# Turning the attention's normalized rows of blocks 2 to 15 on VectorE in squares of 32, from permuted row tiles, with a gather inside SBUF

## The chip, the cores and the metric

The kernel runs on one core of one Trainium2 chip, in float32. The metric is the device time of one execution in microseconds; the time of a kernel is the median of several executions. All five engines of the core are in use: TensorE (PE, with its weight loads PEld), VectorE (DVE), ScalarE (ACT), GpSimd (POOL), and SyncE (SP), which issues nearly all DMAs.

## What is computed

One transformer block with adaptive layer norm, on x of 8 × 1024 × 512 (16 heads of 32) with a condition of 8 × 512. Cut to what matters:

```python
mod = jax.nn.silu(condition) @ Wada + bada
sh_a, sc_a, gt_a, sh_m, sc_m, gt_m = jnp.split(mod, 6, axis=1)
xn = _layernorm(x, g1, be1)
xm = xn * (1.0 + sc_a[:, None, :]) + sh_a[:, None, :]
x = x + gt_a[:, None, :] * _attention(xm, Wqkv, Wproj, bproj)
xn = _layernorm(x, g2, be2)
xm = xn * (1.0 + sc_m[:, None, :]) + sh_m[:, None, :]
h = jax.nn.gelu(xm @ W1 + b1, approximate=False)
x = x + gt_m[:, None, :] * (h @ W2 + b2)
```

The attention is causal. What the change touches is the path from x to the first `xm`: x arrives as rows of tokens, the layer norm's statistics need a token's 512 values in one partition, and the products q, k and v need the 512 values along the partitions. So the normalized rows have to be transposed.

## The kernel before

**Tiling.** The 8192 tokens are 16 blocks of 512, half a sequence each. A block's rows are four row tiles (`hat`, 128 tokens × 512 values), which become four column chunks (`xm[:, c, :]`, 128 values × 512 tokens). The large products (qkv, up, down, proj) use seven products of halves in place of eight; their combinations are named as in the code. Of the attention's input they are B11, B21 and B22 (quarters of `xm`), T1 (written over the fourth quarter) and T2, T3, T4 (three parts of a second tile, `t`). Of a weight they are A11, S1 and so on, 256 KB each. Each of the seven products of a block is 16 matmuls in L205, written as 32 or 64 records in the trace.

**Order.** The kernel writes its own instruction order. A planner runs along while the program is built: it keeps a clock for every engine (`now`), the time at which each piece of data will be there (`written`) and each buffer will be free (`left`). A `note(engine, ns, reads, writes)` advances a clock. `plan` lists the steps of each of the stages; the linear products form the main stream, the attention runs beside it, and side threads opened with `start(...)` are taken up when what they `yield` on is due by the planner's clocks. `either` and `sooner` choose an engine in the same way. On the chip each engine then runs its instructions strictly in that order, each waiting for the semaphores of what it needs. `costs` gives the share of PE's time that a step is expected to take, by which the attention's work is paced.

**Weights.** SP fetches them in a fixed order into a ring of nine tiles `w` (`fetch`, `release`): a fetch goes out when a product releases the tile that it overwrites. In the profile these are L342 (a quarter of a raw weight) and L344 (a sum kept in DRAM). The same queue carries the loads of x (L384 for `hat`, L1230 for the residual) and the stores of the result (L1070).

**The part that is changed.** Step `load_xa` loads four row tiles of a block with four DMAs, `norm_a` takes the statistics (L568 on DVE) and normalizes in place (L594 on ACT; L589 on DVE for two tiles of block 0). Step `at` opens the side thread `modulated`: for each chunk, PE transposes four 128 × 128 squares into a PSUM bank (L656), and DVE (L660) or ACT (L666) applies gain and shift on the way from the bank to `xm`. Then come T1 (L673), T2 (L675) and, through `either` (L162 on DVE, L165 on POOL), T3 and T4. `mt` does the same for the second layer norm, from tiles `xh`, and is not changed. For blocks 2 to 15 `at` stands in the plan behind a part of an up or down product of an earlier block: the attention's input is made ready ahead of its use.

**Around it.** In blocks 4 to 15 the thread runs while the down product of another block ends. Its last combinations on DVE are u2 (then `u2 += b2_rows`), u3 and y21, each the evacuation of one product from its bank (L197). After it come the seven products of v (`project_v`), the first of which, p1, is copied out of its bank by ACT (L192). u3 lives in a buffer of tag "p1", which v's p1 uses next; u3 is read by y21:

```python
u3 = stage("u3", "p1")
combine_out(u3, bank, ps, u2, [key("u2")], [key("u3")])
...
y = stage("y21", "y", 2)
combine_out(y, bank, ps, u3, [key("u3")], [key("y21")])
```

The linear products share three PSUM banks (`lin_bank`); a product needs a bank whose last content was copied out.

Of the kernel before, what the change touches and what calls it, by code (L numbers as in the profile page):

```python
# [9 lines left out]
F32 = mybir.dt.float32  # L10
BF16 = mybir.dt.bfloat16
AF = mybir.ActivationFunctionType
# [10 lines left out]
def kernel(  # L23
# [33 lines left out]
    nc = tc.nc  # L57
    B, T, D = x.shape
    HD = W1.shape[1]
    P = 128  # L60
    hd = D // H
    scale = float(hd) ** -0.5
    TB = 512
    NTT = TB // P
    NHALF = T // TB
    NC = D // P
# [28 lines left out]
    written, left = {}, {}  # L95
# [16 lines left out]
    def note(engine, ns, reads=(), writes=(), port=False):  # L112
        start = max(now[engine], due(reads, writes))
        if port:
            start = max([start] + [b for a, b in pool_spans if a <= start < b])
        end = start + ns
        now[engine] = end
        if engine == "POOL":
            pool_spans.append((start, end))
            del pool_spans[:-16]  # L120
        for k in reads:
            left[k] = max(left.get(k, 0.0), end + SYNC)
        for k in writes:
            written[k] = end + SYNC
        return end

    def note_pe(ns, form, reads=(), writes=()):
        now["PE"] = max(now["PE"], due(reads, writes))
        if shape[0] != form:
            shape[0] = form  # L130
            now["PE"] += SWITCH
        note("PE", ns, reads)
        spent[0] += ns
        for k in writes:
            written[k] = now["PE"] + PIPE

    def note_act(ns, func, reads=(), writes=()):
        if func is not None and table[0] != func:
            table[0] = func
            ns += TABLE  # L140
        note("ACT", ns, reads, writes)
# [5 lines left out]
    def sooner(reads, writes, dve, act):  # L147

        t = due(reads, writes)
        return "DVE" if max(now["DVE"], t) + dve <= max(now["ACT"], t) + act else "ACT"  # L150
# [26 lines left out]
    def lin_bank():  # L177
        i = min(
            (i for i in range(3) if not live[i]),
            key=lambda i: left.get(("l", i), 0.0),  # L180
        )
        live[i] = True
        return i
# [30 lines left out]
    TR = 108  # L214
# [106 lines left out]

    order = [at for w in range(-1, NB + 1) for step in plan[w] for at in pieces_of(step)]
    costs = {"at": 16 * TR, "mt": 16 * TR, "gates": 4 * MM, "mod": 32 * TR}
    costs.update({kind: 14 * MM for kind in ("k", "q", "v", "u", "proj")})

    def planned_time(w):
# [22 lines left out]
    def take(count):  # L349
        i = taken[0]  # L350
        taken[0] += count
        return list(range(i, taken[0]))
# [10 lines left out]
    def halves(i):  # L363
        return piece(i).rearrange("p (k n) -> p k n", n=HB)
# [11 lines left out]
        r0 += n  # L376
    O_G1, O_BE1, O_G2, O_BE2, O_BPROJ, O_B1, O_BADA = at

    def load_x(n, pool, tag):
        b, h = blocks[n]  # L380
        tiles = []
        for t in range(NTT):
            xt = pool.tile([P, D], F32, tag=tag, name=f"{tag}_{n}_{t}", bufs=NTT)
            nc.sync.dma_start(xt, x[b, h * TB + t * P : h * TB + (t + 1) * P, :])  # L384
            tiles.append(xt)
        return tiles

    x_pre = {0: load_x(0, tmp, "hat")}
# [7 lines left out]
        make_causal_mask(nc, mask[:, ts(i, P)], MASKED)  # L396
    eps = const.tile([P, 1], F32, tag="eps", name="eps")
    nc.gpsimd.memset(eps, EPS)
    ones = const.tile([P, P], F32, tag="ones", name="ones")
    nc.gpsimd.memset(ones, 1.0)  # L400
    minus_ones = const.tile([P, P], BF16, tag="minus_ones", name="minus_ones")
    nc.gpsimd.memset(minus_ones, -1.0)
# [66 lines left out]
    def gates(kind):  # L469

        i, bias = GATES[kind]
        at = take(4)
        part = {kf: halves(j) for kf, j in zip(RAW, at)}
        b_gate = tmp.tile([P, D], F32, tag="y", name=f"b_gate_{kind}")[:B, :]
        nc.sync.dma_start(b_gate, bada[i * D : (i + 1) * D].unsqueeze(0).to_broadcast([B, D]))
        if bias is not None:
            b_out = tmp.tile([P, D], F32, tag="y", name=f"b_out_{kind}")[:B, :]
            nc.sync.dma_start(b_out, bias.unsqueeze(0).to_broadcast([B, D]))
        yield [], [BANK]
        bank = lin_bank()  # L480
        ps = banks[bank][:B, :]
        for fh in range(2):
            for k in range(NC):
                if fh + k:
                    yield [], []
                nc.tensor.matmul(
                    ps[:, half(fh, HB)], condT[:, k, :], part[k // 2, fh][:, k % 2, :],
                    start=fh + k == 0, stop=k == NC - 1, skip_group_check=True,
                )
                note_pe(2 * COLUMN * HB, "columns", [], [("l", bank)])  # L490
        release(*at)
        combine_out(b_gate, bank, ps, b_gate)
        made = [(f"g{kind}", b_gate)]
        if bias is not None:
            nc.vector.tensor_tensor(b_out, b_out, b_gate, ALU.mult)
            note("DVE", 700, port=True)
            made.append((f"gb{kind}", b_out))
        for name, row in made:
            kept_rows[name] = kept.tile([B, D], F32, tag=f"kept_{name}", name=f"kept_{name}")
            nc.sync.dma_start(kept_rows[name], row)  # L500
# [11 lines left out]
    def add_job(job, reads, first=False):  # L512

        at = sum(1 for other in jobs if other[2]) if first else len(jobs)
        jobs.insert(at, (job, reads, first))
# [88 lines left out]
    def normalize_tile(xt, key, t, source):  # L604
# [21 lines left out]

        return apply

    def modulated(key, gain, shift, b, guards):
        for t in ("B11", "B21", "B22", "T1", "T2", "T3", "T4"):  # L630
            written[key, t] = NEVER
        yield [("hat", key, 0), *guards], [BANK]
        got = hats.pop(key)
        xm = act.tile([P, NC, TB], F32, tag="xm", name=f"xm_{key}")
        sums = act.tile([P, 3, 2, HB], F32, tag="t", name=f"t_{key}")
        one, two = slice(0, 2), slice(2, 4)
        left_half, right_half = slice(0, HB), slice(HB, TB)
        part = {
            "B11": xm[:, one, left_half],
            "B21": xm[:, two, left_half],  # L640
            "B22": xm[:, two, right_half],
            "T1": xm[:, one, right_half],
            "T2": sums[:, 0, :, :],
            "T3": sums[:, 1, :, :],
            "T4": sums[:, 2, :, :],
        }
        xm_of[key] = part
        at = {t: (key, t) for t in part}
        for c in range(NC):
            if c:  # L650
                yield [("hat", key, 0)], [BANK]
            bank = lin_bank()
            for t in range(NTT):
                if t:
                    yield [("hat", key, t)], []
                nc.tensor.transpose(banks[bank][:, ts(t, P)], got[t][:, ts(c, P)], ident)  # L656
                note_pe(TR, "whole", [("hat", key, t)], [("l", bank)])
            writes = [at["B11"], at["T1"]] if c < 2 else [at["B21"], at["B22"]]
            if sooner([("l", bank)], writes, 770, 780) == "DVE":
                nc.vector.tensor_scalar(  # L660
                    xm[:, c, :], banks[bank], gain[:, c, b : b + 1], shift[:, c, b : b + 1],
                    ALU.mult, ALU.add,
                )
                note("DVE", 770, [("l", bank)], writes)
            else:
                nc.scalar.activation(  # L666
                    xm[:, c, :], banks[bank], AF.Identity,
                    bias=shift[:, c, b : b + 1], scale=gain[:, c, b : b + 1],
                )
                note_act(780, None, [("l", bank)], writes)  # L670
            live[bank] = False
            if c == 1:
                nc.vector.tensor_tensor(part["T1"], part["T1"], part["B11"], ALU.subtract)  # L673
                note("DVE", 700, [at["B11"], at["T1"]], [at["T1"]], port=True)
        nc.vector.tensor_tensor(part["T2"], part["B22"], part["T1"], ALU.subtract)  # L675
        note("DVE", 700, [at["B22"], at["T1"]], [at["T2"]], port=True)
        for out, a, b in (("T3", "T2", "B11"), ("T4", "B21", "T2")):
            either(part[out], part[a], part[b], ALU.subtract, [at[a], at[b]], [at[out]])
# [941 lines left out]
    def finish(n, g):  # L1620
# [7 lines left out]
        for i, (c0, w, term, held) in enumerate(terms):  # L1628
            for j in range(HPG):
                r = slice(j * hd, (j + 1) * hd)  # L1630
                nc.tensor.matmul(  # L1631
                    banks[bank][r, TB - w :], ones[:, :hd], term[:, j, c0 : c0 + w],
                    start=i == 0, stop=i == len(terms) - 1, skip_group_check=True,
                )
            note_pe(2 * COLUMN * w, "columns", [("acc", n, g), ("p", held)], [("l", bank)])
# [234 lines left out]
```

## Time and profile before

| | us |
|---|---|
| median of 3 executions | 3527.01 (3524.73 to 3528.19) |
| the profiled execution, own time | 3526.6 |
| its span, first to last instruction | 3524.9 |
| PE busy in it | 3482.2 |
| DVE, ACT, POOL busy | 1882.3, 1286.5, 2065.1 |
| mean granted PE clock | 0.999 |

A row of a timeline reads: start, duration, engine and line, operation, output <- inputs, count, and in brackets how long the engine stood idle before it and whose end it waited for. Rows of a chain of waits give start, duration and what the chain ran through. A row by line or form gives busy time and mean ns, then the idle time ahead and its releasers; a row for one tile gives shortest, median and longest ns. SPq and ACTq are the queues in which SP and ACT issue DMAs: their durations are those of issuing, not of the transfer. Names of one family are merged: u_d stands for u2, u3 of a down product, p_v for the p's of v.

### The profile page before, as it was taken

The page shows a single profiled execution, that of the slowest core. Times are in us where ns is not written, and L with a number is a line of the kernel's source. Part 1 is how long each engine was busy: PE and PEld are TensorE (multiplying, and loading weights), DVE is VectorE, ACT ScalarE, POOL GpSimd, SP SyncE. Part 2 cuts the span into 40 slices and gives each one's busy share as a digit, 9 for nine tenths or more (in the row PEclk, how much of TensorE's full clock was granted, in tenths as well). Part 3 has the DMA queues.
Part 4 walks back from the last instruction along what each step waited for, and adds up shares of the span by engine and source line. Part 5 has one row for each costly group of instructions (what it writes and reads, how often), then busy time and mean ns, then how long its engine had stood idle before and what let it go on. Part 6 is the DMA issues. An engine that isn't in the chain of part 4 may idle for free.

```text
span 3524.9 us, 123741 instructions
## 1 busy us (share of the span) xinstructions
PE 3482.2 (99%) x56189; PEld 1800.1 (51%) x56189; DVE 1882.3 (53%) x2086; ACT 1286.5 (36%) x1422; POOL 2065.1 (59%) x2205
## 2 busy tenths in 40 slices
PE   7999999999999999999999999999999999999999
PEld 4444455445554554545545455454554545545445
DVE  5765664554635456364563645635446354554463
ACT  2335243352433514235152352514424244241521
POOL 3676755665456664576645766557664576644650
PEclk9999999999999999999999999999999999999999
DMA  6842334334343343533435334353343533434234
GB/s 208 267 143 89 115 109 120 123 106 142 107 139 103 109 142 103 155 100 100 145 99 159 97 103 139 101 157 99 104 139 100 156 101 108 131 100 151 89 118 137
DMA packets 319945, 441.76 MB, mean 125 GB/s; under 512 B 26569, under 2 KB 188677, under 8 KB 319421
## 3 DMA queue, kind: packets, MB, share of 16 engines
q1 hardware_dynamic: 319168, 433.54, 40.2%
q8 instruction: 443, 7.26, 0.8%
q14 instruction: 82, 0.66, 0.1%
q10 hardware_dynamic: 252, 0.29, 0.0%
HBM read 404.32 MB, written 29.41 MB: 123 GB/s over the span
## 4 chain that ended last, share of the span: by engine, by line
PE 93%; DVE 2%; POOL 2%; DMA 1%; issue 1%; ACT 1%; SPq 0%; DVEq 0%; POOLq 0%; ACTq 0%
PE bank L205 64%; PE sc L1476 9%; PE po L1610 7%; PE st L1569 7%; PE st L1557 2%; PE bank L656 2%; DVE mx L1493 2%; PE bank L1631 2%; POOL pT L1695 1%; PE bank L1531 0%; POOL hT L165 0%; DVE sc L1490 0%; DMA w<-in_L_cond_Wada_dram 0%; DMA hat<-in_x_dram 0%; DMA w<-in_L_cond_Wproj_dram 0%
## 5 line engine op out<-in xcount | busy, mean ns | idle before, releaser
L1695 POOL TENSOR_TENSOR pT<-pT,pT 128x256 f32<-128x256 f32 (+3 forms) x1254 | 1179.0, 975 | 202.0 <-ACT pT L1582 115.8
L1582 ACT ACTIVATE pT<-st 128x2048 f32<-128x2048 f32 x288 | 541.1, 1879 | 1046.0 <-PE st L1569 933.0
L205 PE MATMUL bank<-w,hT 128*32 128x256 f32 x14336 | 797.5, 379 | 0.1
L1493 DVE TENSOR_REDUCE mx<-sc 128x4 f32<-128x2048 f32 (+3 forms) x384 | 665.9, 1755 | 133.8 <-PE sc L1476 127.1
L205 PEld LDWEIGHTS bank<-w,hT 128*32 128x32 f32 x14336 | 451.9, 110 | 331.1 <-issue 26.6
L205 PE MATMUL bank<-xm_m,w 128*32 128x256 f32 x8192 | 499.4, 381 | 0.0
L205 PE MATMUL bank<-t_m,w 128*32 128x256 f32 x6144 | 383.9, 380 | 0.0
L205 PEld LDWEIGHTS bank<-xm_m,w 128*32 128x32 f32 x8192 | 252.1, 110 | 242.6 <-issue 80.9
L1587 POOL TENSOR_SCALAR_AFFINE_SELECT pT<-pT 128x512 f32<-128x512 f32 x256 | 165.2, 663 | 326.1 <-ACT pT L1582 324.6
L1476 PE MATMUL sc<-kT,qT 32*128 32x512 f32 (+3 forms) x3072 | 329.1, 520 | 5.7 <-DVE mx L1493 3.1
L1610 PE MATMUL po<-pT,v 128*32 128x512 f32 (+3 forms) x3072 | 305.6, 492 | 3.1 <-POOL pT L1587 3.1
L1490 DVE TENSOR_TENSOR sc<-sc,mask 128x1024 f32<-128x1024 f32 (+1 forms) x160 | 162.9, 1018 | 256.6 <-PE sc L1476 204.1
L1569 PE MATMUL st<-qT,kT 32*128 32x512 f32 (+3 forms) x3072 | 299.9, 486 | 0.0
L205 PEld LDWEIGHTS bank<-t_m,w 128*32 128x32 f32 x6144 | 192.1, 110 | 180.5 <-issue 52.7
L205 PE MATMUL bank<-xm_a,w 128*32 128x256 f32 x3968 | 250.3, 382 | 0.0
L197 DVE TENSOR_TENSOR hT<-bank,u_u 128x512 f32<-128x512 f32 x192 | 129.1, 686 | 158.1 <-PE bank L205 155.9
L165 POOL TENSOR_TENSOR qT<-top,rec 128x512 f32<-128x512 f32 x61 | 78.0, 1278 | 227.5 <-ACT rec L1649 227.5
L1476 PEld LDWEIGHTS sc<-kT,qT 32*128 32x128 f32 x3072 | 129.5, 183 | 155.1 <-ACT pT L1582 63.6
L205 PE MATMUL bank<-w,qT 128*32 128x256 f32 (+1 forms) x2944 | 191.0, 399 | 1.3 <-DMA w<-in_L_cond_Wproj_dram 1.3
L1030 ACT ACTIVATE hT<-hT,cols 128x512 f32<-128x512 f32 x256 | 164.2, 711 | 54.9 <-DVE hT L197 54.3
L205 PE MATMUL bank<-t_a,w 128*32 128x256 f32 x2944 | 183.9, 380 | 0.0
L205 PEld LDWEIGHTS bank<-xm_a,w 128*32 128x32 f32 x3968 | 122.9, 110 | 100.1 <-issue 17.6
(211 smaller groups left out, 3477.8 us busy)
## 6 DMA issues: line engine op xcount, KB each, us to landing
w<-in_L_cond_W_dram SPq DMA_DIRECT2D x384, 256.0 KB
w<-kept_up_S SPq DMA_DIRECT2D x256, 256.0 KB
w<-kept_down_S SPq DMA_DIRECT2D x256, 256.0 KB
w<-kept_qkv_S SPq DMA_DIRECT2D x180, 256.0 KB
w<-in_L_cond_Wqkv_dram SPq DMA_DIRECT2D x147, 256.0 KB
hat<-in_x_dram SPq DMA_DIRECT2D x64, 256.0 KB
xr<-in_x_dram SPq DMA_DIRECT2D x64, 256.0 KB
out_dram<-xr SPq DMA_DIRECT2D x64, 256.0 KB
```

Of the source, the lines that this page charges most:

```text
L165: nc.gpsimd.tensor_tensor(out, a, b, op)
L197: nc.vector.tensor_tensor(out, src, other, op)
L205: nc.tensor.matmul(ps[r, :], lhsT[:, r], rhs, start=start, stop=stop, skip_group_check=True)
L1030: nc.scalar.activation(hT[:, i, :], hT[:, i, :], AF.Gelu, bias=cols[:, O_B1 + f : O_B1 + f + 1])
L1476: nc.tensor.matmul(sc[:, j, c0 : c0 + w], qTs[n][r, gg, ts(qt, P)], keys_of(n, kh)[r, gg, :w], start=True, stop=True, skip_group_check=True,)
L1490: nc.vector.tensor_tensor(place, place, shape_of.to_broadcast(place.shape), ALU.add)
L1493: nc.vector.tensor_reduce(maxima[n, gg][:, kh, qt, :], sc[:, :, c0 : c0 + w], axis=AX.X, op=ALU.max)
L1569: nc.tensor.matmul(st[:, j, c0 : c0 + w], kT[r, gg, ts(k % NTT, P)], qT[r, gg, TB - w :], start=False, stop=True, skip_group_check=True,)
L1582: nc.scalar.activation(pT[:, :, :used], st[:, :, :used], AF.Exp, scale=scale)
L1587: nc.gpsimd.affine_select(diagonal, diagonal, pattern=[[0, HPG], [1, P]], compare_op=ALU.is_ge, fill=0.0, base=0, channel_multiplier=-1,)
L1610: nc.tensor.matmul(po[r, TB - w :], v[:, k % NTT, g * P + j * hd : g * P + (j + 1) * hd], pT[:, j, c0 : c0 + w], start=(k == 0), stop=last ...
L1695: nc.gpsimd.tensor_tensor(into, into, pT[:, j, c0 : c0 + w], ALU.add)
```

## The change

For blocks n > 1 (14 of 16):

- `load_x` fills each row tile with four DMAs of 32 rows in place of one of 128. Tile t, partitions 32a to 32a+31, gets the tokens 128a + 32t to 128a + 32t + 31.
- `normalize` is as before; statistics and normalization don't depend on which token is in which partition.
- `turn_rows` replaces the transposes on PE. Each row tile is turned on DVE in squares of 32 × 32, by two instructions: column chunks 0 to 2 go to the tile `t` (the room of T2, T3 and T4, not yet written), chunk 3 to a new tile `turn`. These are jobs of DVE's job list, one a row tile. After the last, SP issues 32 DMAs within SBUF: 16 of 32 partitions × 3 × 128 values and 16 of 32 partitions × 128 values. Each moves 512-byte runs into their partitions of `xm`. The planner notes 720 ns of DVE a row tile and sets the landing of all to 6000 ns after DVE's clock.
- `modulated` for these blocks takes no bank: gain and shift are applied in place on `xm`, by DVE (planner's cost 500 ns) or ACT (780 ns), after the planner's landing time. T1 to T4 follow as before.
- `costs["at"]` becomes 0, `gates` yields once more ahead of its loads, and `ones` shrinks from 128 × 128 to 128 × 32.

In the built program 224 transposes leave PE; 112 square turns on DVE, 448 DMAs of the gather and 168 more loads of x are added. In blocks 4 to 15 DVE's order is: one row tile's two turns, u2, the b2 add, six turns, u3, apply of chunk 1, T1, apply of chunk 3, T2, T3, y21, then v's evacuations; ACT has the applies of chunks 0 and 2, then v's p1. SP has a weight fetch, the 32 gather DMAs, then the next weight fetch. A DMA issued by SP also waits for the DMA eight before it, since eight semaphores are used in turn.

```diff
@@ costs
     costs = {"at": 16 * TR, "mt": 16 * TR, "gates": 4 * MM, "mod": 32 * TR}
+    costs["at"] = 0
@@ load_x
+    SQ = 32
+
+    def is_turned(n):
+        return n > 1
+
     def load_x(n, pool, tag):
...
             xt = pool.tile([P, D], F32, tag=tag, name=f"{tag}_{n}_{t}", bufs=NTT)
-            nc.sync.dma_start(xt, x[b, h * TB + t * P : h * TB + (t + 1) * P, :])
             tiles.append(xt)
+            if not is_turned(n):
+                nc.sync.dma_start(xt, x[b, h * TB + t * P : h * TB + (t + 1) * P, :])
+                continue
+            for a in range(P // SQ):
+                r0 = h * TB + a * P + t * SQ
+                nc.sync.dma_start(xt[a * SQ : (a + 1) * SQ, :], x[b, r0 : r0 + SQ, :])
@@ constants
-    ones = const.tile([P, P], F32, tag="ones", name="ones")
+    ones = const.tile([P, hd], F32, tag="ones", name="ones")
@@ gates
+        if tail_key[0] is not None:
+            yield [tail_key[0]], []
@@ new
+    def turn_rows(key, tiles, xm, sums):
+
+        def turn(t):
+            source = tiles[t].rearrange("p (c j r) -> p c j r", c=NC, r=SQ)
+            for c0, c1, to in parts:
+                nc.vector.transpose(
+                    to[:, :, :, t, :].rearrange("p c j r -> p (c j) r"),
+                    source[:, c0:c1, :, :].rearrange("p c j r -> p (c j) r"),
+                )
+            note("DVE", 720, [("hat", key, t)], [])
+            if t == NTT - 1:
+                for c0, c1, to in parts:
+                    for a in range(P // SQ):
+                        for j in range(P // SQ):
+                            nc.sync.dma_start(
+                                xm[j * SQ : (j + 1) * SQ, c0:c1, a * P : (a + 1) * P],
+                                to[a * SQ : (a + 1) * SQ, :, j, :, :].rearrange("p c t r -> p c (t r)"),
+                            )
+                written["spread", key] = now["DVE"] + 6000
+
+        rest = tmp.tile([P, 1, P // SQ, NTT, SQ], F32, tag="turn", name=f"turn_{key}", bufs=1)
+        first = sums.rearrange("p c i n -> p (c i n)").rearrange(
+            "p (c j t r) -> p c j t r", c=3, t=NTT, r=SQ
+        )
+        parts = ((0, 3, first), (3, 4, rest))
+        written["spread", key] = NEVER
+        for t in range(NTT):
+            add_job(lambda t=t: turn(t), [("hat", key, t)])
@@ modulated
-        yield [("hat", key, 0), *guards], [BANK]
+        rows_turned = key[0] == "a" and is_turned(int(key[1:]))
+        yield [("hat", key, 0), *guards], [] if rows_turned else [BANK]
...
+        if rows_turned:
+            turn_rows(key, got, xm, sums)
+            yield [("spread", key)], []
         for c in range(NC):
...
+            if rows_turned:
+                if c:
+                    yield [("spread", key)], []
+                rows, source, on_dve = xm[:, c, :], ("spread", key), 500
+            else:
...
+                rows, source, on_dve = banks[bank], ("l", bank), 770
+            if sooner([source], writes, on_dve, 780) == "DVE":
                 nc.vector.tensor_scalar(
-                    xm[:, c, :], banks[bank], gain[:, c, b : b + 1], shift[:, c, b : b + 1],
+                    xm[:, c, :], rows, gain[:, c, b : b + 1], shift[:, c, b : b + 1],
                     ALU.mult, ALU.add,
                 )
...
                 nc.scalar.activation(
-                    xm[:, c, :], banks[bank], AF.Identity,
+                    xm[:, c, :], rows, AF.Identity,
                     bias=shift[:, c, b : b + 1], scale=gain[:, c, b : b + 1],
                 )
```

More of the change, by code (lines that the diff above doesn't have):

```diff
@@ L648, in modulated @@
         at = {t: (key, t) for t in part}
+        if rows_turned:
+            turn_rows(key, got, xm, sums)
+            yield [("spread", key)], []
         for c in range(NC):
[L650 to L657, printed above, removed]
@@ L658, in modulated @@
-            writes = [at["B11"], at["T1"]] if c < 2 else [at["B21"], at["B22"]]
-            if sooner([("l", bank)], writes, 770, 780) == "DVE":
+            writes = [at["B11"], at["T1"]] if c < 2 else [at["B21"], at["B22"]]
+            if rows_turned:
[3 more added lines that the diff above has]
+            else:
+                if c:
+                    yield [("hat", key, 0)], [BANK]
+                bank = lin_bank()
+                for t in range(NTT):
+                    if t:
+                        yield [("hat", key, t)], []
+                    nc.tensor.transpose(banks[bank][:, ts(t, P)], got[t][:, ts(c, P)], ident)
+                    note_pe(TR, "whole", [("hat", key, t)], [("l", bank)])
+                rows, source, on_dve = banks[bank], ("l", bank), 770
@@ L660, in modulated @@
+            if sooner([source], writes, on_dve, 780) == "DVE":
                 nc.vector.tensor_scalar(
-                    xm[:, c, :], banks[bank], gain[:, c, b : b + 1], shift[:, c, b : b + 1],
+                    xm[:, c, :], rows, gain[:, c, b : b + 1], shift[:, c, b : b + 1],
                     ALU.mult, ALU.add,
                 )
-                note("DVE", 770, [("l", bank)], writes)
+                note("DVE", on_dve, [source], writes, port=rows_turned)
             else:
                 nc.scalar.activation(
-                    xm[:, c, :], banks[bank], AF.Identity,
+                    xm[:, c, :], rows, AF.Identity,
@@ L668, in modulated @@
                     bias=shift[:, c, b : b + 1], scale=gain[:, c, b : b + 1],
                 )
-                note_act(780, None, [("l", bank)], writes)
-            live[bank] = False
+                note_act(780, None, [source], writes)
+            if not rows_turned:
+                live[bank] = False
             if c == 1:
@@ L1631, in finish @@
                 nc.tensor.matmul(
-                    banks[bank][r, TB - w :], ones[:, :hd], term[:, j, c0 : c0 + w],
+                    banks[bank][r, TB - w :], ones, term[:, j, c0 : c0 + w],
                     start=i == 0, stop=i == len(terms) - 1, skip_group_check=True,
```

## The prediction, made before the changed kernel had run

> **What bounds the kernel now.** I read the page first: busy shares, the chain that ended last, the clock.
>
> ```profile
> span 3524.9 us, 123741 instructions
> ...
> PE 3482.2 (99%) x56189; PEld 1800.1 (51%) x56189; DVE 1882.3 (53%) x2086; ACT 1286.5 (36%) x1422; POOL 2065.1 (59%) x2205
> ...
> PEclk9999999999999999999999999999999999999999
> ...
> PE 93%; DVE 2%; POOL 2%; DMA 1%; issue 1%; ACT 1%; SPq 0%; DVEq 0%; POOLq 0%; ACTq 0%
> ```
>
> PE is busy in 99% of the span at a full granted clock in every slice. So the time is PE's work plus about 42 us in which it waits (3524.9 − 3482.2). Work taken from PE is worth its full length; any new wait of PE costs its full length. DVE at 53% has room on average, but that says nothing of its order.
>
> Then the groups by form on PE, and the chain of waits around the place where block 7's rows are turned (1225 to 1300 us):
>
> ```profile
> L656 PE MATMUL bank<-ident,hat 128*128 128x128 f32 x256 | 36.9, 290 | 2.1 <-ACT xm_a L666 2.1
> ```
> ```profile
> 1243.23 5.18 PE bank L205 x96
> 1248.41 2.11 PE bank L656 x16
> 1250.53 0.01 issue
> 1250.54 34.31 PE bank L205 x632
> ```
>
> The 256 transposes are 16 for each of 16 blocks; the change removes 14 × 16 = 224. In block 7 they stand as one run of 16 that holds the chain for 2.12 us, and behind it comes a stretch of 34.31 us with nothing but L205 products: the rest of block 4's down product, then v of block 6. The new work of the change falls into that stretch.
>
> **What it removes.** The ceiling is 14 runs × 2.12 = 29.7 us. The floor goes by the weight loads of the same run alone:
>
> ```profile
> 1248.34 1.30 PEld L656 LDWEIGHTS bank<-ident,hat 128*128 128x128 f32 x12 [0.41 <-issue]
> ```
>
> 1.30 / 12 = 0.108 us each, × 224 = 24.3. I take 27, the middle. The four reads of a PSUM bank (L666) become four SBUF applies; they free no PE time.
>
> **What it adds on DVE: the turns.** Eight 32×32-square transposes a block, two to a row tile (384 and 128 elements a lane). In the changed program's DVE order one pair stands before the evacuation u2 of the down product, the other three right after u2's b2 add, then u3, then the new applies. The rows of before at those places:
>
> ```profile
> 1254.42 0.68 DVE L673 TENSOR_TENSOR xm_a<-xm_a 128x512 f32<-128x512 f32 x1
> 1255.21 0.69 DVE L675 TENSOR_TENSOR t_a<-xm_a 128x512 f32<-128x512 f32 x1
> 1255.94 0.69 DVE L162 TENSOR_TENSOR t_a<-xm_a,t_a 128x512 f32<-128x512 f32 x1
> ...
> 1259.80 0.69 DVE L162 TENSOR_TENSOR u_d<-u_d,b_rows 128x512 f32<-128x512 f32 x1 [1.39 <-POOL v_d L165]
> ...
> 1261.17 3.77 SPq L344 DMA_DIRECT2D w<-kept_qkv_S  x3
> ...
> 1264.63 0.69 DVE L197 TENSOR_TENSOR u_d<-bank,u_d 128x512 f32<-128x512 f32 x1 [4.14 <-PE bank L205]
> ...
> 1271.53 0.69 DVE L197 TENSOR_TENSOR y_d<-bank,u_d 128x512 f32<-128x512 f32 x1 [6.21 <-PE bank L205]
> ...
> 1273.30 0.59 ACT L192 COPY p_v<-bank 128x512 f32<-128x512 f32 x1 [21.48 <-PE bank L205]
> ...
> 1274.74 3.64 PE L205 MATMUL bank<-w,xm_a 128*32 128x256 f32 x64
> ```
> ```profile
> L384 SPq DMA_DIRECT2D hat<-in_x_dram x64: 327/382/924, 1.3 to 2879.8; - x64
> L568 DVE BATCH_NORM_STATS2 st_a<-hat x64: 659/663/685, 8.3 to 2928.8; 128x6 f32<-128x512 f32 x64
> ...
> L589 DVE TENSOR_SCALAR hat<-hat,rstd_a,offset_a x2: 537/542/548, 12.5 to 13.0; 128x512 f32<-128x512 f32 x2
> ```
>
> I keep the clock of before; PE's 2.12 us shift moves all of it alike. The trace has no transpose on DVE. One pair moves 512 elements a lane, as the rows of 0.54 (one SBUF input) and 0.69 do, with one more start: I take 0.74. From 1259.80 + 0.69 = 1260.49, three pairs end at 1262.7. The bounds are 0.54 and, if a square costs each element twice, 1.5 a pair (1265.0). The Trainium skill, VectorE: DVE Perf Modes, section The three transpose paths, gives 311 ns for a 128×128 bf16 turn in squares; an estimate from it, four to a row tile, is 1.24 us, three would end at 1264.2, and the sum below would grow by 0.9 us a block, 12 in all. No run so far shows it.
>
> **What it adds on SP: the spread.** 32 DMAs a block, all in SP's queue, in the changed order directly behind a weight fetch that is the second of the three at 1261.17. Those three go out one L205 product apart (the third ends at 1264.94, starts about 0.39 earlier, and the one before 1.72 earlier, about 1262.85). So the second has been issued at 1263.3; the turns are done, and the spread starts there, S = 1263.3. How far apart do 32 DMAs leave? Nothing in before is a DMA within SBUF. The nearest rows, from two windows of the timeline:
>
> ```profile
> 713.19 1.81 SPq L384 DMA_DIRECT2D hat<-in_x_dram  x4
> ...
> 1.66 0.32 ACTq L374 DMA_DIRECT2D rows<-in_L_cond_g_dram  x1
> ...
> 2.01 0.32 ACTq L374 DMA_DIRECT2D rows<-in_L_cond_be_dram  x1
> ...
> 3.29 0.30 ACTq L374 DMA_DIRECT2D rows<-in_L_cond_bada_dram  x1
> ...
> 4.86 0.36 ACTq L404 DMA_DIRECT2D b_rows<-in_L_cond_b_dram  x1
> 5.25 1.28 ACT L413 ACT_TABLE_LOAD   x1 [5.25 <-DMA rows<-in_L_cond_b_dram]
> ...
> 9.70 0.72 POOL L405 TENSOR_TENSOR b_rows<-b_rows 128x256 f32<-128x256 f32 x1 [6.98 <-DMA b_rows<-in_L_cond_b_dram]
> ```
>
> Large ones: (1.81 − 0.38) / 3 = 0.477 start to start. Small ones: 2.01 − 1.66 = 0.35. The spread's are 48 and 16 KB, between them: i = 0.41. For the landing, the last small one of 3.29 had landed by 5.25: L = 2.0 (up to 2.5 counted from the earlier issues); the 256 KB broadcast took 9.70 − 4.86 = 4.84, the far bound.
>
> The last spread DMA lands at S + 31i + L = 1263.3 + 12.7 + 2.0 = 1278.0. DVE's order behind it is fixed: apply of chunk 3 (0.54 + 0.06), T2, T3, then the evacuation y21 (0.75 each with its gap, by the rows at 1254 to 1256). y21 was at 1271.53 and now stands behind the applies. ACT's copy of p1 of v writes y21's operand u3's buffer, so it waits for y21 (0.1 gap, 0.59), and a later product of v needs the bank which that copy empties. In before that product went at 1274.74. Now: 1263.3 + 31i + 2.0 + 0.6 + 2.25 + 0.1 + 0.59 = 1268.84 + 31i. PE's new wait a block is **31i − 5.9 = 6.8 us**. At i = 0.35 it is 4.95, at 0.477 it is 8.9; each 0.5 us of landing adds 0.5. This arrangement is the same in blocks 4 to 15: 12 × 6.8 = 81.6. In block 3 ACT makes all four applies and p1's copy is behind them, about 1 us shorter: 5.8.
>
> The planner reckons the spread as landed 6 us after the last turn; by these rows it is 31i + L = 14.7 us. This is the step that carries the forecast.
>
> **What else is moved.** The weights behind the burst: the fetch released by u3's product at about 1264.6 goes out at S + 32i = 1276.4, and lands some 2.5 later, about 1279; its product comes about 13.8 us (eight products of 1.72) after the release, 1278.4. Alone that would cost 1 us or, with the 4.84 landing, 3; behind PE's wait of 6.8 it costs nothing. The row tiles come in 16 DMAs instead of 4: 12 × 0.41 = 5 us more of SP a block, covered by the queue's idle time:
>
> ```profile
> SPq L344 <- PE bank L205: 1436.8, 676, 12.4
> SPq L342 <- PE bank L205: 1084.6, 489, 7.5
> ```
> ```profile
> 40.00:270.00 230.00, 221.71 (x3560) 111.99 (x3556) 165.41 (x180) 81.69 (x92) 136.38 (x156) 1.00 0.60 195
> ```
>
> SP waits 2521 us of the span for PE to release a ring tile. Only early on is the queue full (the second fence: from 40 to 270 us PE is busy 221.71 of 230, and the DMA share is 0.60): for block 2, whose spread stands ahead of two weight fetches, I take 2.5 us (0 to 6), and for the split loads there 2 (−2 to 4). The smaller `ones` tile and the extra yield of `gates` cost nothing: one is a shape in SBUF, the other runs before the main stretch.
>
> **The sum**, on the profiled execution: 3524.9 − 27 + 81.6 + 5.8 + 2.5 + 2 = 3589.8 of span; that execution took 3526.6 with 3524.9 of span, against a median of 3527.0, so 2 us lie around it: **3592**. At i = 0.35 with the ceiling of the gain: 3524.9 − 29.7 + 59.4 + 4 − 2 + 2 = 3559. At i = 0.477 with the floor, 0.5 more landing and the upper ends early on: 3524.9 − 24.3 + 106.7 + 7.9 + 6.9 + 10 + 2 = 3634.
>
> **The rivals.**
> A. The spread keeps up: DMAs of 32 rows leave SP so fast that the last lands before y21 is late. That needs 31i below 5.9, i below 0.19 us; then only the gain is left, 3527 − 27 = 3500, faster. For it: a DMA of 32 rows has a quarter of a row tile's rows, and SP is idle there. Against it: the shortest of 64 issues took 0.327, the ACT's with four rows or fewer 0.30 to 0.32. Chance 0.06.
>
> B. DVE's order doesn't bind (y21's buffer is not the one that p1 needs, or the applies come sooner), and only the weights behind the burst are late: 1 to 3 us in 13 blocks, with the 4.5 early on, 3500 + 13 to 39 + 4.5, about 3530. For it: the ring is what SP's waits are made of. Against it: in order on DVE nothing passes the apply. Chance 0.06.
>
> C. The turns hold up SP: from 0.94 us a pair ((1263.3 − 1260.49) / 3) each further 0.1 moves S by 0.3. At 1.5 S is 1.7 later, 13 × 1.7 = 22, 3614; at 2.2, what an add on two SBUF inputs takes beside POOL, 3.8 later, 3641.
>
> ```profile
> L162 DVE TENSOR_TENSOR y_d<-y_d,row_gm 128x512 f32<-128x512 f32 x17 | 37.5, 2207 | 0.1
> ```
>
> For it: POOL's adds run in that stretch. Against it: the statistics (L568), which read one SBUF input, stay within 659 to 685 whatever POOL does. Chance 0.12, at 3628.
>
> D. The spread is bound by its DMAs, not by their issue: each waits for the one eight before it, so with 4.84 of landing i becomes 4.84 / 8 = 0.605, and the wait 31 × 0.605 + 2.84 − 5.9 = 15.7 a block, 13 × 15.7 = 204: about 3708. Decides from a landing above 8 × 0.41 = 3.3. For it: 32 partitions at a time in 512-byte runs, beside weights. Against it: seven small DMAs from 0.80 to 3.29 had all landed by 5.25. Chance 0.08. The Trainium skill, DMA: Bandwidth & Descriptors, section Rules for kernel authors, speaks for this side: under 64 KB a transfer is mostly overhead, and many should become one. By the 0.68 us that its table of measurements has for 4 KB, one behind another, an estimate is 31 × 0.68 − 5.9 = 15 us a block.
>
> **How the numbers follow.** The forecast has 0.68, its own range is 3559 to 3634. What this kernel's measurement tells from no change is about 0.2%, 7 us. Faster by more: A, with a little of B, 0.07; within: the rest of B's lower half, 0.04; slower: forecast, C, D and B's upper half, 0.89. For 8 in 10 the range reaches over C and over B's middle: 3530 to 3650; A and D stay out.
>
> **What would show it.** In the changed profile: PE waiting once a block, 5 to 9 us, before L205 on xm_a (block's v), put down to ACT's copy of p_v, and that to DVE's y_d; SP with 32 issues at 0.35 to 0.48 in a row; L712 on DVE waiting for the DMA into xm_a; turns (L647) of some 0.25 and 0.5 us; L656 of before at 32 transposes for blocks 0 and 1. PE's busy time should fall to about 3455 while the span rises. Wrong: if PE's waits are on weights (B), if L647's mean pair is over 0.94 (C), if the issues stand over 0.5 apart (D), or if there is no wait behind the apply (A).

## The result, and the profile after

The changed kernel takes 3730.01 us (median of 5, 3728.2 to 3734.56) against 3526.93 (median of 5): a ratio of 1.058, 95% interval 1.057 to 1.060. It is slower by 203 us, far above the range that was forecast (3530 to 3650), on the side that was forecast. The profiled execution took 3734.56 with a span of 3732.8.

The page of the changed kernel:

```profile
span 3732.8 us, 124495 instructions
...
PE 3485.5 (93%) x55965; PEld 1778.8 (48%) x55965; DVE 1927.7 (52%) x2216; ACT 1272.6 (34%) x1400; POOL 2067.2 (55%) x2209
...
PE 85%; SPq 7%; DVE 3%; issue 1%; DMA 1%; POOL 1%; ACT 1%; DVEq 0%; ACTq 0%; POOLq 0%
PE bank L205 58%; PE sc L1529 8%; SPq L656 7%; PE po L1663 7%; PE st L1622 6%; PE st L1610 2%; DVE mx L1546 2%; PE bank L1684 1%; PE bank L708 1%; DMA xm_a<-turn_a 1%; PE bank L1584 0%; POOL pT L1748 0%; DMA w<-in_L_cond_Wada_dram 0%; DVE sc L1543 0%; PE bank L499 0%
```

Two things stand out. PE waits 247 us of the span (3732.8 − 3485.5), 205 more than before, and a new line has come into the chain: SP's issuing of the gather DMAs (L656), 7%. And PE is not less busy, though 224 transposes are gone: 3485.5 against 3482.2. The waits by engine and line say whom PE waits for, and whom that one waits for:

```profile
PE bank L205 <- ACT p_v L192: 192.0, 13, 16.0
...
ACT p_v L192 <- DVE y_d L197: 136.0, 12, 11.5
```

That is the pair that the prediction named, in 13 blocks, but 14.8 us each in place of 6.8. The timeline of one block (7) shows the whole of it:

```profile
1329.09 0.27 DVE L647 STREAM_TRANSPOSE turn_a<-hat 128x128 f32<-128x128 f32 x1
...
1330.21 12.10 SPq L656 DMA_DIRECT2D xm_a<-t_a  x16
1331.56 0.69 DVE L197 TENSOR_TENSOR u_d<-bank,u_d 128x512 f32<-128x512 f32 x1 [2.20 <-issue]
...
1342.41 10.06 SPq L656 DMA_DIRECT2D xm_a<-turn_a  x16
...
1352.57 0.53 SPq L345 DMA_DIRECT2D w<-kept_qkv_S  x1
...
1353.75 0.55 DVE L712 TENSOR_SCALAR xm_a<-xm_a,gaina,shifta 128x512 f32<-128x512 f32 x1 [8.48 <-DMA xm_a<-turn_a]
...
1354.40 0.69 DVE L728 TENSOR_TENSOR t_a<-xm_a 128x512 f32<-128x512 f32 x1
...
1355.12 0.69 DVE L162 TENSOR_TENSOR t_a<-xm_a,t_a 128x512 f32<-128x512 f32 x1
...
1355.73 0.68 DVE L197 TENSOR_TENSOR y_d<-bank,u_d 128x512 f32<-128x512 f32 x1
1356.53 0.58 ACT L192 COPY p_v<-bank 128x512 f32<-128x512 f32 x1 [11.28 <-DVE y_d L197]
...
1357.16 6.50 PE L205 MATMUL bank<-w,xm_a 128*32 128x256 f32 x64 [15.37 <-ACT p_v L192]
```

SP issues 32 DMAs from 1330.21 to 1352.47 without a break. The 16 larger ones took 2 us more than the 16 smaller ones only because two of them took 1.90 and 1.09 us; the others stand some 0.64 us apart, whatever their size. Every burst has one to four issues of 0.7 to 1.9 us, and no run shows what makes them long. Only then can DVE apply chunk 3, make T2 and T3, and come to y21 (y_d), for which ACT's copy waits, for which PE waits: 15.37 us. The last row holds a second loss: the product behind the wait (64 records) takes 6.50 us; before it took 3.64. Windows of PE's busy time and granted clock (the column ahead of the last two) around it:

```profile
1338.00:1342.00 4.00, 3.80 (x72) 2.03 (x64) 0.00 (x0) 0.00 (x0) 0.00 (x0) 1.00 0.35 77
1342.00:1346.00 4.00, 0.00 (x0) 0.00 (x0) 1.24 (x2) 1.52 (x2) 0.00 (x0) 0.99 0.19 42
1346.00:1357.00 11.00, 0.00 (x0) 0.00 (x0) 2.53 (x4) 0.47 (x1) 1.83 (x2) 0.50 0.35 104
1357.00:1363.00 6.00, 5.83 (x56) 2.76 (x60) 0.69 (x1) 0.70 (x2) 3.66 (x3) 0.50 0.89 299
1363.00:1367.00 4.00, 4.00 (x80) 2.21 (x76) 1.38 (x2) 0.00 (x0) 0.00 (x0) 1.00 0.56 184
```

Some 4 us into the wait the granted clock falls to 0.50, and it stays there for the first 6 us of work. That is why PE's busy time did not fall to the forecast 3455. In the groups by form (columns as before):

```profile
L205 PE MATMUL bank<-w,xm_a 128*32 128x256 f32 x1984 | 144.1, 447 | 192.0 <-ACT p_v L192 192.0
...
L708 PE MATMUL bank<-ident,hat 128*128 128x128 f32 x32 | 6.1, 354 | 1.7 <-ACT xm_a L718 1.7
...
L499 PE MATMUL bank<-w,condT 128*8 128x256 f32 x32 | 10.1, 476 | 15.1 <-DVE v L197 15.1
```

The transposes went from 36.9 to 6.1 us (−30.8), and the product behind the wait from 116.5, its busy time in the kernel before, to 144.1 (+27.6). With the waits on p_v (192.0) and one of 15.1 us in the early part (L499), 3524.9 − 30.8 + 27.6 + 192.0 + 15.1 = 3728.8 of the 3732.8.

### The profile page after: what moved, and what is told of

It reads as the page before. It is cut to its first block, busy times and chain, and to the rows that moved or that the text cites. A ratio compares the mean times of both kernels' runs of the same rounds, so it can differ in the third digit from the quotient of the medians.

```text
span 3732.8 us, 124495 instructions
## 1 busy us (share of the span) xinstructions
PE 3485.5 (93%) x55965; PEld 1778.8 (48%) x55965; DVE 1927.7 (52%) x2216; ACT 1272.6 (34%) x1400; POOL 2067.2 (55%) x2209
## 4 chain that ended last, share of the span: by engine, by line
PE 85%; SPq 7%; DVE 3%; issue 1%; DMA 1%; POOL 1%; ACT 1%; DVEq 0%; ACTq 0%; POOLq 0%
PE bank L205 58%; PE sc L1529 8%; SPq L656 7%; PE po L1663 7%; PE st L1622 6%; PE st L1610 2%; DVE mx L1546 2%; PE bank L1684 1%; PE bank L708 1%; DMA xm_a<-turn_a 1%; PE bank L1584 0%; POOL pT L1748 0%; DMA w<-in_L_cond_Wada_dram 0%; DVE sc L1543 0%; PE bank L499 0%
## 5 line engine op out<-in xcount | busy, mean ns | idle before, releaser
L205 PE MATMUL bank<-w,xm_a 128*32 128x256 f32 x1984 | 144.1, 447 | 192.0 <-ACT p_v L192 192.0
L205 PEld LDWEIGHTS bank<-w,xm_a 128*32 128x32 f32 x1984 | 70.0, 128 | 259.7 <-ACT p_v L192 198.0
```

Source lines behind the costliest of these rows:

```text
L205: nc.tensor.matmul(ps[r, :], lhsT[:, r], rhs, start=start, stop=stop, skip_group_check=True)
```

## The experiments

Eleven variants of the changed kernel that ran beside the kernel before, and one that undoes its main part. The first four ask which wait it is, and whether the DMAs' number sets it.

**Applies put off** (e1): `written["spread", key] = now["DVE"] + 24000` in place of 6000.

> Only the planner's landing time is changed, 24000 ns after the last turn in place of 6000, so that DVE's order has y21 and the evacuations of v ahead of the four applies; the 32 gather DMAs stay one unbroken burst on SP. Theory (the order on DVE makes PE wait; behind it stands a second wait, on the weight fetch behind the burst): the waits of PE on ACT's copy of p_v go to under 10 us in all, and PE waits on weights instead: the fetch leaves 22 us after S, lands 2.7 later, its product comes 13.8 after the release, so 10 us a block, 13 x 10 = 130, with the half clock after each wait (2.9 x 13 = 37) on 3500: about 3665. Rival 1 (only the order on DVE matters, the ring has room): about 3500. Rival 2 (the DMAs inside SBUF slow the core whatever the order): no change, about 3730.

3759.17 us, 1.066 (1.064 to 1.068). PE no longer waits for p_v, and the second wait has come out:

```profile
PE bank L205 <- DMA w<-kept_qkv_S: 150.4, 17, 15.1
```

Block by block it is 10 to 15 us. So the mechanism is as the theory has it: under the wait for DVE's order lies one for the weight fetch that stands behind the burst in SP's queue, and curing the first alone gains nothing. It came out 94 us above the estimate. The waits on weights are 20 us more than its 130 (14.4 to 15.1 us in every second block from 1800 us on). Most of the rest, some 64 us, is small new waits, the longest 7.3 us, many of them for the attention's work on DVE, among which the applies now fall.

**The whole burst in pairs between weight fetches** (e2). Two pending DMAs leave behind each fetch:

```diff
             ring.append(w)
+            trickle(2)
```

> The same turns and the same 32 gather DMAs a block, but two of them go out behind each weight fetch, and the applies come 4 us after the last pair by the planner's clock. Theory (the burst in one piece and the fixed order behind it are the whole cost; the turns and the DMAs by themselves cost PE nothing): PE's waits on p_v and on weights both go, and the time is that of before less PE's work: 3493 to 3505. Rival (448 more DMAs, 168 more loads and 112 turns cost by themselves, through the queue or the ports): above 3527.

3656.64 us, 1.037 (1.035 to 1.038). A miss: the waits on p_v and on weights are gone, but the time is not. The windows show where it went:

```profile
180.00:270.00 90.00, 63.20 (x486) 24.25 (x486) 45.17 (x81) 27.76 (x19) 69.31 (x74) 0.84 0.21 75
270.00:360.00 90.00, 73.68 (x949) 35.34 (x950) 40.90 (x63) 24.57 (x26) 56.58 (x59) 0.88 0.22 66
...
1000.00:2000.00 1000.00, 978.06 (x15824) 498.80 (x15816) 541.01 (x609) 373.77 (x411) 574.42 (x619) 1.00 0.42 122
```

Between 90 and 450 us PE is idle for 65 us (9 in the kernel before), at a granted clock of 0.84 to 0.93: few fetches go out there, so the DMAs don't either, and the products that need `xm` stand still. Later PE is idle 22 us in 1000 (2 before), most of it in waits for the attention's DVE work, among which the applies now fall. The variant changed the order of much besides the burst, so it did not decide between the theory and its rival.

**17 DMAs in place of 32** (e3): `nc.sync.dma_start(xm[:, 3, :], rest...)` once, the loop over chunk 3's part left out.

> The 16 gather DMAs of chunk 3 are replaced by one of 128 partitions x 2 KB, the other 16 stay: 17 DMAs a block with the same bytes. Chunk 3's values land in a wrong order, nothing else is left out. Theory (the number of issues by 0.70 us sets the wait): 16 x 0.70 - 5.9 = 5.3 us of PE wait a block, 69 over 13 blocks, on 3500: about 3569, and up to 3606 if PE's clock also halves after so short a wait. Rival (the transfers, by bytes or by landing, set it): the wait stays near 15 us, 3700 or more.

3621.56 us, 1.027 (1.025 to 1.028). With the same bytes the wait on p_v falls by half, to 90.3 us over 13 blocks, 6.9 each: the number of issues sets it, not the bytes. The estimate of 5.3 was short for two reasons. Over blocks 4 to 15 the 17 stood 0.73 us apart, 11.75 from the first to the last; and since the last DMA is now one of chunks 0 to 2, the apply of chunk 1 and T1 stand behind it too, 1.44 us on DVE. With both, 11.75 + 1.44 − 5.9 = 7.3, and that is the mean wait of these blocks. After so short a wait the clock falls as well (in block 7 to 0.50 from some 5 us on, for 3 us of work).

**All blocks on PE again, the rest kept** (e4): `return n > NB` in `is_turned`.

> No block is turned on DVE (the transposes of all blocks on PE again, loads of 128 rows), but the rest of the change stays: cost 0 of the step in the planner, the extra yield of the gates, the smaller ones tile. Theory: this rest is worth nothing, 3527 within 7. Rival (part of the loss is the changed pacing): clearly above 3534.

3529.21 us, 1.000 (0.999 to 1.001): the cost of 0, the yield and the smaller `ones` are worth nothing.

The next three take the issue apart.

**Chunk 3's 16 DMAs on ACT's queue** (e5): `(nc.scalar if c0 else nc.sync).dma_start(`.

> The 16 gather DMAs of chunk 3 are issued by ACT, the other 16 by SP as in the change; nothing else differs. Theory (each queue issues one such DMA in 0.64 us, and the two queues issue side by side): the last gather DMA goes out about 16 x 0.70 = 11 us after S, PE's wait is 15 x 0.70 - 5.9 = 4.6 us a block with 2.4 us of slowed PE behind it, as with 17 DMAs: about 3600 (3585 to 3625). Rival (both queues share what makes an issue long): the wait stays near 15 us, about 3730.

3677.86 us, 1.043 (1.040 to 1.045); waits on p_v 124.8 us over 12 blocks, 10.4 each, between the two theories. The timeline of one block:

```profile
1314.45 12.00 ACTq L656 DMA_DIRECT2D xm_a<-turn_a  x16
1316.22 14.77 SPq L656 DMA_DIRECT2D xm_a<-t_a  x16
```

Side by side, SP's 16 take 14.77 us and ACT's 12.00, against 12.10 and 10.06 one after the other on SP alone. The queues do work at once: 32 issues in 16.5 us rather than 22.3, but not in 11. The median issue is as long as before (0.597 us on SP, 0.603 on ACT). What SP adds is waiting:

```profile
SPq L656 <- DMA xm_a<-turn_a: 57.4, 53, 3.4
```

SP's and ACT's DMAs now take turns on the same eight semaphores, so SP waits until a DMA of ACT has landed before it issues its own. In this block that is 3.7 us: the semaphore of SP's second DMA was complete at 1317.85, and that DMA left at 1317.87. The Trainium skill, DMA: Bandwidth & Descriptors, section Issuing engines are not separate DMA queues, says that a second issuing engine saves only the sequencer's time. Here that time was the bound, and the second queue saved 5.8 us of it, about half of what two independent queues would have. Separate semaphores for the two were not tried.

**Two queues, and the applies put off** (e6), e5 and e1 together.

> As with two queues, and the applies put off in the planner by 24000 ns in place of 6000. Theory (two waits in a row: the order on DVE, then the weight fetch behind the burst; each has to go): the fetch leaves 11.2 us after S and lands by 14, at the 13.8 us after the release that its product allows, so at most 1 to 2 us of wait a block: 3500 to 3530. Rival (the loss has a third part, the turns or the DMAs' traffic): above 3560.

3665.18 us, 1.039 (1.037 to 1.041): a miss. The wait on weights falls to 32.1 us and that on p_v to 20.5, far below e1's and e5's, though together 4 us a block where the theory had 1 to 2. What else is left lies in the early part and in the attention, as in e2: between 90 and 180 us PE is busy 70.55 of 90 (85.23 in the kernel before), and between 1000 and 2000 us 957.67.

**The gather reads DRAM** (e7): the source of the same 32 DMAs is `x[0, ...]` of the same shape.

> The change, but each of the 32 gather DMAs reads rows of x in DRAM of the same shape (32 x 3 x 128 or 32 x 128 values) in place of the turned tiles, so the values are others. Theory (an issue is longer because the source lies in SBUF): as the loads of 32 rows from DRAM, 0.53 apart, the wait is 31 x 0.53 - 5.9 = 10.5 us and the time about 3670. Rival (it is the destination, or the 32-partition shape with 512-byte runs): 0.64 apart, about 3730.

The 16 KB DMAs read pieces of 512 bytes as before, the 48 KB ones 1536 bytes in a row. 3662.29 us, 1.038 (1.036 to 1.041). The row of the line, and those of the changed kernel for comparison (shortest, median, longest ns of one issue):

```profile
L656 SPq DMA_DIRECT2D xm_a<-in_x_dram x448: 310/423/1900, 129.0 to 3131.9; - x150
```
```profile
L656 SPq DMA_DIRECT2D xm_a<-t_a x224: 585/597/1898, 131.6 to 3195.6; - x112
L656 SPq DMA_DIRECT2D xm_a<-turn_a x224: 507/589/1701, 143.0 to 3205.8; - x112
...
DMA to landing us min/median/max: 1.7/1.9/4.2
```

From DRAM one issue takes 0.42 us, from SBUF 0.60, whether it moves 48 KB or 16 KB. 32 in a row took 16.43 us from DRAM, 0.516 apart, and the wait was 123.9 / 13 = 9.5 us against 31 × 0.516 − 5.9 = 10.1. With DRAM as the source most of the issue's extra length is gone; the landing is short. But a source in SBUF alone does not make an issue long. The stores of the result, from SBUF to DRAM, and the one DMA of 128 partitions within SBUF in e3 show it:

```profile
L1123 SPq DMA_DIRECT2D out_dram<-xr x62: 337/396/1217, 403.1 to 3725.3; - x62
```
```profile
L653 SPq DMA_DIRECT2D xm_a<-turn_a x14: 542/542/565, 132.6 to 3081.2; - x14
```

The issues of 0.54 to 0.60 us are those with both ends in SBUF; one end in DRAM, on either side, goes with about 0.4. Why was not tried.

The last five ask whether the turns and DMAs cost anything by themselves. **Timed, one step earlier** (e8): a list of pending DMAs is emptied by PE's planned clock, and `at` stands one part of the down product earlier:

```diff
+        while pending and now["PE"] >= gather_at[0]:
+            gather_at[0] += 1200
+            pending.pop(0)()
...
-                late = m[3:6] + at + m[6:]
+                late = m[3:5] + at + m[5:]
```

> The step that turns a block stands one part of the down product earlier in the plan; the 32 gather DMAs leave SP one at a time by the planner's PE clock, 1.2 us apart, between the weight fetches; the applies come 3 us after the last. Theory (burst and order are the whole cost): PE's waits on p_v and on weights go without the attention being disturbed as it was with pairs behind the fetches, 3495 to 3515, faster than before. Rival (turns on DVE and DMAs cost by themselves): above 3527.

3591.05 us, 1.018 (1.016 to 1.020): a miss, though half of the loss of e2 is gone. The applies had come to stand between two evacuations of v, and PE waits for those:

```profile
PE bank L210 <- DVE u_v L202: 21.1, 8, 4.6
PE po L1679 <- ACT top L1713: 15.4, 6, 2.6
```

**0.9 us apart, blocks 2 and 3 on PE** (e9) and **1.0 us apart** (e10).

> As the timed version before it, with two differences: blocks 2 and 3 keep their transposes on PE, so that the crowded start is as before the change, and the gather DMAs leave 0.9 us apart by the planner's clock, so that the applies fall between u3 and y21 (4 to 6 us in which DVE idles) and not among v's evacuations. Theory (burst and order are the cost; turns, DMAs and their traffic cost PE nothing where DVE and SP have room): 12 x 2.1 = 25 us less PE work, against waits of 0 to 20 us in the attention that the planner's new order brings (24 us in the version before it): 3500 to 3525, at or below the kernel before. Rival (turns and DMAs cost by themselves): above 3545.

> As the 0.9 us version with 1.0 us between the gather DMAs: SP has 0.36 us left between two of them for its weight fetches in place of 0.26, and the applies of the odd blocks fall behind v's second evacuation. Theory: if SP's queue still delays weights at 0.9, this one is faster; if the applies among v's evacuations cost, it is slower by 6 blocks x 1.6 to 4 us = 10 to 25 us. Rival (turns and DMAs cost by themselves): both alike, above 3545.

3539.02 us, 1.004 (1.002 to 1.005), and 3568.31, 1.012 (1.010 to 1.013). e9 lies above what the theory allowed, below what its rival asked for; e10 is 29 us slower than e9, a little more than the 10 to 25 expected. In e10, where the applies of the odd blocks stand among v's evacuations, such waits come in nearly every block, 2.6 to 5.3 us each. PE's new waits in e9 are one in two blocks, 27.8 us for p_v in all, and the timeline shows each to hang on the last gather DMA again, which leaves at 1265.39 and later, behind two stores (and one of the last two issues here is a long one, 2.57 us):

```profile
1264.52 0.82 SPq L1137 DMA_DIRECT2D out_dram<-xr  x2
...
1265.39 3.21 SPq L665 DMA_DIRECT2D xm_a<-turn_a  x2
...
1271.07 0.55 DVE L726 TENSOR_SCALAR xm_a<-xm_a,gaina,shifta 128x512 f32<-128x512 f32 x1 [9.08 <-DMA xm_a<-turn_a]
...
1274.48 5.94 PE L210 MATMUL bank<-w,xm_a 128*32 128x256 f32 x64 [5.04 <-ACT p_v L197]
```

**8 of them on ACT** (e11) and **16 on ACT** (e12), otherwise as e9: `queue = nc.scalar if c0 and j % 2 else nc.sync`, then `if c0`.

> As the 0.9 us version, but 8 of the 32 gather DMAs of a block (every second of chunk 3's) are issued by ACT, which idles 14 us there. In the 0.9 us version PE still waits once in two blocks, 4.0 to 5.0 us (27 us in all, with slowed PE behind it), because SP's last gather DMAs leave 3 to 5 us after the planner's time. Theory: 8 issues fewer on SP, 8 x 0.64 = 5 us, end that lateness; left is the gain of 25 us and under 10 us of new waits: 3503 to 3515, faster than before. Rival (turns, DMAs and the changed order keep costing PE): 3525 or more.

> As the version with 8 gather DMAs on ACT, now with all 16 of chunk 3 there. In that version the last gather DMA of every second block still left SP behind two stores of the result that wait for POOL, and PE waited 1.9 to 2.7 us for it. Theory: on ACT's queue no store is ahead of it, and these waits (11.6 us by the profile) go: 3505 to 3514. Rival (ACT's issues hold up its own copies and applies by as much): 3518 or more.

3520.01 us, 0.998 (0.997 to 0.999), and **3494.28 us, 0.991 (0.989 to 0.993)**. e11 lies above the theory's range and below the rival's, e12 11 us below the theory's range: from e11 to e12 not only the 11.6 us of waits went, PE's busy time fell as well, from 3464.1 to 3454.7. With the last DMAs out of the queue in which stores and fetches wait, PE's waits on p_v are gone, and the page is as before but for the work that was taken off:

```profile
span 3494.5 us, 124339 instructions
...
PE 3454.7 (99%) x55997; PEld 1777.6 (51%) x55997; DVE 1955.1 (56%) x2199; ACT 1280.0 (37%) x1408; POOL 2077.8 (59%) x2202
```

12 blocks turned: PE's busy time falls by 3482.2 − 3454.7 = 27.5 us, 2.3 a block, PE's waits by 3, and DVE's 73 us more (1955.1 against 1882.3) cost nothing. This is faster than both kernels. For these 12 blocks it settles the rival that the turns or the DMAs cost PE by themselves; e9 to e12 leave blocks 2 and 3 on PE, so it says nothing of the early part.

## Why the prediction was wrong, step by step

- **What bounds the kernel** and **the new wait's place** were right: PE's work is the time, and the chain gather DMA, apply of chunk 3, T2, T3, y21, copy of p1, product of v ended last in each of blocks 4 to 15.
- **The wait's formula**, 31i − 5.9, was right: with the i of the trace, (1351.88 − 1330.21) / 31 = 0.70 (the last issue's start less the first's), it gives 15.8; the trace has 15.37 in block 7.
- **The step that failed is i = 0.41**, "the spread's are 48 and 16 KB, between them". Both rows were of DMAs from DRAM to SBUF, and size was taken as what orders them. Size does nothing (0.597 and 0.589 us an issue for 48 and 16 KB); that both ends lie in SBUF goes with the length (0.42 from DRAM in e7, 0.40 to DRAM in the stores). Both ends that were given, 0.35 and 0.477, came from the same kind of row, so the true 0.70 lay outside them: 0.64 for most issues, and the rest from the long ones. This term was 82 us in the sum and is 192 − 10 (block 3) = 182.
- **A term was missing**: PE's clock at half for 3 to 6 us of work behind each long wait, 27.6 us. The sum put nothing in for it. The page of before has a 9 for the clock in every slice, but a finer window of its trace shows the fall once, behind a wait of 2.70 us near the end (the column ahead of the last two):

```profile
3420.90:3424.20 3.30, 3.30 (x21) 2.74 (x24) 1.50 (x2) 2.00 (x3) 0.00 (x0) 0.50 0.03 5
```

The Trainium skill has it, TensorE: Matmul & The Clock Gate, Part 1: The HAM clock gate: half rate after an idle window of about 3.4 us, full rate again after as long a busy one. The trace agrees in kind: over the 14 long waits 2.3 to 5.2 us of idling until the fall and 2.6 to 6.0 us of work until the return, and each stretch at 0.50 is three, four or five times 3.41 us long. Where they differ the measurement decides: waits of 2.1 to 2.7 us, shorter than such a window, were enough in the kernel before and in e11.

- **The gain** was 30.8 us of transposes, above the 29.7 that was given as the ceiling (e12: 2.3 us a block against 2.12). The 2.12 was block 7's run alone; the row of all 256 transposes that the prediction shows gives 36.9 / 16 = 2.3 a block.
- **Early on**, 2.5 us for block 2 became 15.1, and not for a late weight as forecast: DVE's evacuations of v (the last row) stand behind T2 (the first row), T3 and T4 of block 2, which wait for the gather, and PE (L499) waits for the bank. (T2's bracket names a store that landed about then; ACT's apply of chunk 3, behind the gather, ended at 156.93.) It is the same wait as in the later blocks, overlooked there.

```profile
156.97 0.69 DVE L728 TENSOR_TENSOR t_a<-xm_a 128x512 f32<-128x512 f32 x1 [8.32 <-DMA kept_up_S<-prep_up]
...
158.91 1.28 DVE L197 TENSOR_TENSOR v<-bank,u_v 128x512 f32<-128x512 f32 x2
```

- **The turns** took 0.55 + 0.27 = 0.82 us a pair (0.74 forecast, below the 0.94 from which they would matter). **The weights behind the burst** were hidden behind the longer wait, as forecast; e1 showed them.
- **The rivals.** D came nearest in time (3708) and had its sign, issues over 0.5 apart, but not its mechanism: even the longest landing, 4.2 us (median 1.9), is shorter than eight issues took here, 8 × 0.64 = 5.1, so SP did not wait for the DMA eight before. SP's issuing itself was the length. A and C fell with i and with the turns' duration; B's wait was there, but second.
- **Two slips** in the working changed nothing: the upper sum has 6.9 us for the later landing, where 13 × 0.5 is 6.5, and the issue of 0.30 us that speaks against A had 24 rows, not four or fewer.

## What to carry to other kernels

Before work goes from the bounding engine to DMAs, count their issues on one queue, ask what stands behind them in that queue and behind their consumer in its engine's order, and take the price of an issue from a row with the same source and the same destination (the stores from SBUF to DRAM, 0.40 us, would have misled as well); if no row has it, leave the range open upward. A wait in a fixed order can have a second wait under it: here DVE's order, the weight fetch behind the burst and the stores ahead of its tail had each to go before the gain of 27 us showed.

## What the runs showed of the hardware that was not expected

- One DMA issue of 32 partitions into SBUF took 0.60 us with SBUF as source and 0.42 with DRAM; within SBUF 48 KB and 16 KB took the same. From SBUF to DRAM an issue took 0.40. On two queues at once (e5) the issues kept their length, and 32 came to 0.52 us a DMA over both against 0.70 on one.
- Of the five PE waits of 1.9 to 2.7 us for p_v in e11, three were followed by 3.4 us at a clock of 0.50 and two left it at 1.00; the rows show one of each, behind waits of 2.12 and 1.93 us. Waits of 3.7 to 5.0 us (e9) all brought it to 0.50, and it came back after 3 to 6 us of work. In e9 a wait of 5.04 us was followed by a product of 5.94 in place of 3.64, so it cost PE 7.3; the wait of 15.37 in block 7 cost 18.2 by the same sum.

```profile
1702.90:1706.20 3.30, 3.30 (x36) 1.67 (x32) 0.59 (x1) 0.58 (x1) 2.35 (x2) 0.50 0.53 190
2132.00:2138.00 6.00, 4.07 (x80) 2.22 (x76) 2.17 (x4) 1.87 (x3) 4.34 (x3) 1.00 0.89 283
```

- The 32 × 32 turns of 384 and 128 elements a lane took 0.55 and 0.27 us:

```profile
L647 DVE STREAM_TRANSPOSE t_a<-hat 128x384 f32<-128x384 f32 x56 | 31.0, 553 | 0.0
...
L647 DVE STREAM_TRANSPOSE turn_a<-hat 128x128 f32<-128x128 f32 x56 | 15.1, 269 | 0.0
```
